# A gated scan after an attention layer: where its roots, step weights and limits are computed

## The chip, the core and the metric

The kernel runs on one core of a Trainium2 chip. A core has a matrix engine (TensorE, PE in the profile, with PEld for its weight loads), a vector engine (VectorE, DVE), an activation engine (ScalarE, ACT), a general engine (GpSimd, POOL), and queues that issue transfers (here SyncE's, SPq, and GpSimd's). Each engine works off its own list in order; engines wait for each other by semaphores. The metric is the device time of one execution in microseconds (us), lower is better. One execution was also recorded by the hardware profiler; the views quoted here are of that one.

## What is computed

Two layers, each added to its input x (8 sequences of 1024 tokens, 512 wide). The first is an attention with 16 heads whose weights are modulated by a condition; it is not touched by the change. The second, cut to what matters:

```python
xr, gate = jnp.split(x @ W_in.T, 2, axis=-1)          # 1024 wide each
xc = silu(conv4(xr + t_emb) + b_conv)                 # causal, four taps, each channel by itself
xn = (xc - mu) / jnp.sqrt(var + 1e-05) * ln_g + ln_b
Bm, Cm, dt = jnp.split(xn @ W_xproj.T, 3, axis=-1)    # 16 states
dt = jnp.tanh(dt @ W_dt.T + b_dt) * 0.01
Ad = 1.0 + dt * (-jnp.tanh(A_log))
Bd = Bm * jnp.minimum(jnp.linalg.norm(xn, axis=-1, keepdims=True), 1.0)
def step(h, inputs):                                  # over 1024 tokens
    ad, bd, xt, ct = inputs
    h = jnp.clip(h * ad[:, :, None] + bd[:, :, None] * xt[:, None, :], -10.0, 10.0)
    return h, jnp.einsum('bd,bdh->bh', ct, h)
y = ys + D * xn
out = x + y * silu(gate) @ W_out.T
```

## The kernel before, in words

**The first layer** (lines 33 to 481) fills the first 3408 us. **The second layer** is `gated_scan`, lines 543 to 1033. The scan state h has 128 partitions (8 sequences times 16 states) and 1024 columns. The kernel keeps h divided by the running product of the decays, so that one step is one VectorE operation (`step`, L933): h plus the step's input, held between two limits that also are divided by that product. The step's input is a row of xn, spread over the 16 states, times a weight of the partition (`st["ws"]`); the output weight is `st["cp"]`.

**Chunks and slots.** Tokens go in 32 chunks of 32 steps; a chunk has two token tiles i = 0, 1 of 16 steps times 8 sequences. All work around the steps is entered in a plan by hand: `at(p0 + k, f, ...)`. For chunk c, p0 is the first step of chunk c-1. So **slot k** below 32 runs in step k of the chunk before, and slots 32 to 63 in the chunk's own steps; the code of one slot is recorded just after `step` of it. Within a slot the work of the older chunk is recorded first, then that of the younger, then `fetch`, `products` and last `weigh`. So step 28 of a chunk holds slot 28 of the next chunk, slot 60 of its own and slot 92 of the one before, and the convolution of the chunk after the next.

**What one chunk does**, by slot: the projection and convolution (`conv_mm`, `conv_in`, `conv_taps`, `conv_out`, slots -12 to 9, that is steps 20 to 31 and 0 to 9; tile `in_ps`, L668 and L672; `xr` L679, `xc` L681, taps L688, `xs` L695); transposes, statistics and the layer norm (`flip_mm` to `scale`, 8 to 17); the root of the variance (`deviation`, 12 and 16); `xt` written to memory (`spill`); norms (`squares`, `lengths`); the projections to B, C and dt (`p_mm` 16, `params` 18, `params_mm` 19 and 21, `params_out` 20 and 22); their spreading by eight small GpSimd transfers (`spread` 24); tanh, running product, weights and limits (`decay` 28); the block of output weights of each tile (`weights` 31 and 41). Then, during its own steps, the gate (`gate_mm`, tile `g_ps`, L823), every four steps the output product (`products`, tile `y_ps`, L920), the gating (`gate_y` L837, `skip` L755), and the last projection (`out_flip` tile `gt_ps`, `out_mm` tile `o_ps`, `out_store`, `out_send`).

**The inputs of the steps.** A tile `xb` holds four steps' inputs. Those of steps 4 to 31 are fetched from memory with a broadcast (`fetch`, 8 transfers of 256 KB, L901). Those of steps 0 to 3 come from TensorE: `fan_mm` (slots 21 and 25) spreads four rows of `xt` into four banks of PSUM for each half of the columns, and `fan_out` (23, 24, 29, 30) copies them to `xb` by ScalarE (L892). Then `weigh(n)` multiplies each step's input by its weight on ScalarE (L911), recorded two steps ahead of its step.

**Buffers.** `xb` has three; h has six, so that step n can write only when `products` has read step n-6; PSUM has two banks for `y_ps` (one tile, 1024 columns) and six, under one tag, for every other product: `in_ps`, `x_ps`, `xp_ps`, `fan_ps`, `g_ps`, `gt_ps`, `o_ps` and more. A product that finds no free bank waits on TensorE until ScalarE or VectorE has read the tile that held it, and all products behind it wait too.

Of the kernel before, what the change touches and what calls it, by code (L numbers as in the profile page):

```python
# [8 lines left out]
F32 = mybir.dt.float32  # L9
BF16 = mybir.dt.bfloat16  # L10
AF = mybir.ActivationFunctionType
ALU = mybir.AluOpType
# [4 lines left out]
P = 128  # L17
B = 8
# [7 lines left out]
TC = 32  # L26
# [516 lines left out]
def gated_scan(ctx, tc, const, tok, x1_d, S, win, tables, w_conv, b_conv, ln_g, ln_b, b_dt, a_log,  # L543
# [69 lines left out]
            ps[:, hf * 512 : (hf + 1) * 512], ident, ident[:, 0:1].to_broadcast([P, 512]), start=True, stop=True  # L613
        )

    eps = wp.tile([P, 1], F32, name="eps_i")
    nc.vector.memset(eps, EPS)
    nc.scalar.activation(na, na, AF.Tanh)
    nc.vector.tensor_scalar_mul(na, na, -0.01)

# [5 lines left out]
    zero = pts[0][:, NX : NX + TC]  # L626
    yws = []
    for n in range(2):
        yw = (tok, wp)[n].tile([P, TT, 4 * B], F32, tag=("sr", "yw")[n], name=f"yw{n}")
        nc.vector.memset(yw, 0.0)  # L630
        yws.append(yw)

# [17 lines left out]
    def at(n, f, *args):  # L650
        if args and args[0] is sts[0] and n < -2:
            n -= 16
        plan.setdefault(n, []).append(lambda: f(*args))
# [73 lines left out]
    def deviation(st, i):  # L727

        rs = st["rs", i] = two.tile([P, 2], F32, name=f"rs{i}")
        mv = st["mv", i]  # L730
        nc.scalar.activation(rs[:, 0:1], mv[:, 1:2], AF.Sqrt, bias=eps)
        nc.vector.reciprocal(rs[:, 0:1], rs[:, 0:1])
        nc.vector.scalar_tensor_tensor(rs[:, 1:2], mv[:, 0:1], -1.0, rs[:, 0:1], ALU.mult, ALU.mult)

    def scale(st, i):
        xt, rs = st["xt", i], st["rs", i]
# [19 lines left out]

    def lengths(st):
        nf = st["nr"] = two.tile([P, NT], F32, name="nr")
        nc.vector.tensor_add(nf, st["nf"][:, :, 0], st["nf"][:, :, 1])
        nc.vector.tensor_scalar_min(nf, nf, 1.0)  # L760
        nc.scalar.activation(nf, nf, AF.Sqrt)

    def params(st, i):
        rs = st["rs", i]
        pt = st["p", i] = pts[i][:, 0:NX]
        add = one.tile([P, NX], F32, name="p_add")
        nc.vector.scalar_tensor_tensor(add, wgs, rs[:, 1:2], wb, ALU.mult, ALU.add)
        nc.vector.scalar_tensor_tensor(pt, st["pt_ps"][:, i, 0:NX], rs[:, 0:1], add, ALU.mult, ALU.add)
        nc.vector.tensor_scalar_mul(pt[:, 0:NS], pt[:, 0:NS], st["nr"][:, i : i + 1])
# [18 lines left out]
    def decay(st):  # L788
        bd, cm, ad = (st["bca"][:, n] for n in range(3))
        nc.scalar.activation(ad, ad, AF.Tanh, bias=bdt)  # L790
        nc.vector.tensor_scalar(ad, ad, na, 1.0, ALU.mult, ALU.add)
        pp = two.tile([P, TC], F32, name="pp")
        nc.vector.tensor_tensor_scan(
            pp, ad, zero, 1.0 if last["p"] is None else last["p"], ALU.mult, ALU.add
        )
        last["p"] = pp[:, TC - 1 : TC]
        lim = st["lim"] = two.tile([P, 2, TC], F32, name="lim")
        nc.vector.reciprocal(lim[:, 0], pp)
        st["ws"] = two.tile([P, TC], F32, name="ws")
        nc.vector.tensor_mul(st["ws"], bd, lim[:, 0])  # L800
        st["cp"] = two.tile([P, TC], F32, name="cp")
        nc.vector.tensor_mul(st["cp"], cm, pp)
        nc.vector.tensor_scalar_mul(lim[:, 1], lim[:, 0], -10.0)
        nc.vector.tensor_scalar_mul(lim[:, 0], lim[:, 0], 10.0)

    def weights(st, i):

        for q in range(4):
            nc.vector.tensor_mul(
                yws[i][:, 4 * q : 4 * q + 4, q * B : (q + 1) * B],  # L810
                my_sb.unsqueeze(1).to_broadcast([P, 4, B]),
                st["cp"][:, i * TT + 4 * q : i * TT + 4 * q + 4].unsqueeze(2).to_broadcast([P, 4, B]),
            )

    def order(st, i):
        xo = st["xo", i] = x1p.tile([P, KH, P], F32, name="x1t")
# [60 lines left out]
    def fan_mm(st, half):  # L877

        for r in range(4):
            ps = st["fan", r] = ps_m.tile([P, 512], F32, tag="mm", name="fan_ps")  # L880
            nc.tensor.matmul(
                ps, sel[32 * r : 32 * r + 32], st["xt", 0][32 * r : 32 * r + 32, half * 512 : (half + 1) * 512],
                start=True, stop=True,
            )

    def fan_out(st, c, half, rs):
        if half == 0 and rs[0] == 0:
            st["xb"] = xbp.tile([P, 4, DI], F32, name="xb")
            for r in range(4):
                xbs[c * TC + r] = st["xb"][:, r]  # L890
        for r in rs:
            nc.scalar.copy(st["xb"][:, r, half * 512 : (half + 1) * 512], st.pop(("fan", r)))  # L892

    def fetch(g):

# [17 lines left out]
    def products(g):  # L913

        c, t = divmod(4 * g, TC)
        i, q = divmod(t // 4, TT // 4)
        st = sts[c]
        for hf in range(2):
            for r in range(4):
                nc.tensor.matmul(  # L920
                    st["y", i][32 * r : 32 * r + 32, hf * 512 : (hf + 1) * 512],
                    yws[i][:, 4 * q + r, :],
                    hs[4 * g + r][:, hf * 512 : (hf + 1) * 512],
                    start=False, stop=(q == 3), skip_group_check=True,
                )
        for r in range(4):
            del hs[4 * g + r]
# [12 lines left out]
    for c in range(NCH):  # L940
        st, n0 = sts[c], c * TC
        p0 = n0 - TC
        if c > 0:
            at(p0 + -20 if c > 1 else -34, load_x1, st, c)
        at(p0 + -15, begin, st)
        for k in range(KI):
            at(p0 + -12 + 2 * k, conv_mm, st, k)
            at(p0 + -11 + 2 * k, conv_in, st, k)
            at(p0 + -10 + 2 * k, conv_taps, st, k, (0,))
            at(p0 + -9 + 2 * k, conv_taps, st, k, (1,))  # L950
            at(p0 + -8 + 2 * k, conv_taps, st, k, (2,))
            at(p0 + -7 + 2 * k, conv_out, st, k)
        at(p0 + 8, flip_mm, st, 0, 0)
        at(p0 + 8, flip_mm, st, 0, 1)
        at(p0 + 11, stats, st, 0, 0)
        at(p0 + 11, stats, st, 0, 1)
        at(p0 + 11, center, st, 0)
        at(p0 + 12, deviation, st, 0)
        at(p0 + 14, scale, st, 0)
        at(p0 + 17, spill, st, 0)  # L960
        at(p0 + 15, squares, st, 0)
        at(p0 + 35, skip, st, 0)
        at(p0 + 12, flip_mm, st, 1, 0)
        at(p0 + 12, flip_mm, st, 1, 1)
        at(p0 + 15, stats, st, 1, 0)
        at(p0 + 15, stats, st, 1, 1)
        at(p0 + 15, center, st, 1)
        at(p0 + 16, deviation, st, 1)
        at(p0 + 17, scale, st, 1)
        at(p0 + 28, spill, st, 1)  # L970
        at(p0 + 18, squares, st, 1)
        at(p0 + 51, skip, st, 1)
        at(p0 + 21, fan_mm, st, 0)
        at(p0 + 23, fan_out, st, c, 0, (0, 1))
        at(p0 + 24, fan_out, st, c, 0, (2, 3))
        at(p0 + 25, fan_mm, st, 1)
        at(p0 + 29, fan_out, st, c, 1, (0, 1))
        at(p0 + 30, fan_out, st, c, 1, (2, 3))
        at(p0 + 16, p_mm, st)
        at(p0 + 18, lengths, st)  # L980
        at(p0 + 18, params, st, 0)
        at(p0 + 19, params_mm, st, 0)
        at(p0 + 20, params_out, st, 0)
        at(p0 + 18, params, st, 1)
        at(p0 + 21, params_mm, st, 1)
        at(p0 + 22, params_out, st, 1)
        at(p0 + 24, spread, st)
        at(p0 + 28, decay, st)
        at(p0 + 31, weights, st, 0)
        at(p0 + 41, weights, st, 1)  # L990
        at(p0 + 34, order, st, 0)
        at(p0 + 36, gate_mm, st, 0, 0)
        at(p0 + 42, gate, st, 0, 0)
        at(p0 + 41, gate_mm, st, 0, 1)
        at(p0 + 43, gate, st, 0, 1)
        at(p0 + 50, gate_y, st, 0)
        at(p0 + 62, out_flip, st, 0, 0)
        at(p0 + 64, out_copy, st, 0, 0)
        at(p0 + 65, out_mm, st, 0, 0)
        at(p0 + 63, out_flip, st, 0, 1)  # L1000
        at(p0 + 65, out_copy, st, 0, 1)
        at(p0 + 69, out_mm, st, 0, 1)
        at(p0 + 73, out_store, st, 0)
        at(p0 + 76, out_send, st, c, 0)
        at(p0 + 46, order, st, 1)
        at(p0 + 49, gate_mm, st, 1, 0)
        at(p0 + 51, gate, st, 1, 0)
        at(p0 + 61, gate_mm, st, 1, 1)
        at(p0 + 64, gate, st, 1, 1)
        at(p0 + 65, gate_y, st, 1)  # L1010
        at(p0 + 68, out_flip, st, 1, 0)
        at(p0 + 68, out_copy, st, 1, 0)
        at(p0 + 77, out_mm, st, 1, 0)
        at(p0 + 70, out_flip, st, 1, 1)
        at(p0 + 77, out_copy, st, 1, 1)
        at(p0 + 78, out_mm, st, 1, 1)
        at(p0 + 80, out_store, st, 1)
        at(p0 + 91, out_send, st, c, 1)
# [2 lines left out]
            at(4 * g - 9 if g > 2 else -25, fetch, g)  # L1021
        at(4 * g + 4, products, g)
    for n in range(S):
        at(n - WA, weigh, n)

    sts[0]["x1"] = x1_now
    last["h"] = hp.tile([P, DI], F32, tag="h", name="h")
# [117 lines left out]
```

## Time and profile before

| | us |
|---|---|
| time before, median of 3 runs | 5712.75 (5705.14 to 5713.35) |
| the profiled execution's own time | 5708.03 |
| its span, first to last instruction | 5706.3 |
| first layer, up to the first scan step | 3408.0 |
| a chunk of 32 steps, mean of chunks 0 to 30 | 71.39 |
| one undisturbed chunk (the 19th, from 4764.57) | 71.08 |

The page gives busy time as a share of the whole span, over both layers. Only the second layer is of interest here, and there the engines stand at: PE 98%, DVE 94%, ACT 89%, transfers 88% (the stretch from 4408 to 5408 us: 981.53, 944.41 and 894.25 us of 1000). GpSimd is busy 123 us of those 1000. A line of the timeline reads: start, length, engine, line of the code, operation, out<-in, shape, count; in brackets the idle time before it and what ended that.

### The profile page before, as it was taken

How to read it: one execution, taken by the hardware profiler on the slowest of the kernel's cores; microseconds unless marked ns; L12 is line 12 of the kernel's file. 1: busy time of each engine (PE TensorE's matmuls, PEld its weight loads, DVE VectorE, ACT ScalarE, POOL GpSimd, SP SyncE). 2: the span in 40 equal slices, each digit the busy share in tenths (PEclk: the TensorE clock that was granted, in tenths of full speed). 3: DMA queues.
4: the chain of work that ended last, by engine and by line, in shares of the span. 5: the costliest groups of instructions: out<-in, count | busy, mean ns of one | idle time of the engine just before them, and what ended most of it. 6: DMA issues, size and time to landing. Idle time of an engine off the chain costs nothing.

```text
span 5706.3 us, 113668 instructions
## 1 busy us (share of the span) xinstructions
PE 5525.4 (97%) x43312; PEld 3178.8 (56%) x43312; DVE 4382.9 (77%) x6874; ACT 3959.9 (69%) x6995; POOL 1540.4 (27%) x1667
## 2 busy tenths in 40 slices
PE   7999999999999999999999989999999999999998
PEld 4565656656556556656556555555555555555553
DVE  4666666766766766766666659999999999999996
ACT  5565655655655655655655558898988888888886
POOL 2343433433434434434433310111111111111111
PEclk9999999999999999999999989999999999999999
DMA  2102212112112112112021248888888888888886
GB/s 83 35 24 64 53 44 67 31 55 57 31 58 53 38 50 67 24 53 71 18 65 41 71 123 233 236 238 237 238 238 234 237 235 238 235 238 236 238 238 188
DMA packets 377216, 714.85 MB, mean 125 GB/s; under 512 B 198320, under 2 KB 280512, under 8 KB 347488
## 3 DMA queue, kind: packets, MB, share of 16 engines
q1 hardware_dynamic: 346704, 684.81, 44.4%
q0 software_dynamic: 29968, 22.77, 1.5%
q8 instruction: 344, 5.64, 0.4%
q14 instruction: 200, 1.64, 0.1%
HBM read 596.66 MB, written 83.89 MB: 119 GB/s over the span
## 4 chain that ended last, share of the span: by engine, by line
PE 63%; DMA 15%; DVE 9%; ACT 8%; issue 3%; SPq 2%; POOL 0%; DVEq 0%; ACTq 0%; POOLq 0%
PE mm_ps L130 17%; PE t_ps L296 15%; DMA xb<-xd 10%; PE s_ps L286 9%; PE t_ps L303 8%; DVE h L933 4%; PE in_ps L668 4%; PE y_ps L920 3%; ACT xb L911 2%; PE g_ps L823 2%; SPq L901 2%; DMA out<-o_sb 2%; ACT pr L457 2%; PE o_ps L860 1%; DMA xd<-xt 1%
## 5 line engine op out<-in xcount | busy, mean ns | idle before, releaser
L447 DVE TENSOR_REDUCE nmax<-s_ps 128x1 f32<-128x1024 f32 x1024 | 1206.2, 1220 | 460.7 <-PE s_ps L289 459.9
L454 ACT COPY pT<-t_ps 128x512 f32<-128x512 f32 x1024 | 550.3, 589 | 1298.9 <-PE t_ps L296 1298.4
L933 DVE CUSTOM_DVE_ANT_0 h<-h,xb,lim 128x1024 f32<-128x1024 f32 x1024 | 1373.5, 1341 | 90.0 <-ACT xb L911 41.2
L296 PEld LDWEIGHTS t_ps<-ident,pr 128*128 128x128 f32 x8192 | 912.2, 141 | 658.9 <-issue 491.7
L911 ACT ACTIVATE xb<-xb,ws 128x1024 f32<-128x1024 f32 x1024 | 1177.8, 1164 | 60.2 <-DMA xb<-xd 45.0
L457 ACT ACTIVATE pr<-s_ps,nmax 128x1024 f32<-128x1024 f32 x1024 | 1139.5, 1127 | 5.0 <-DVE nmax L447 4.8
L296 PE MATMUL t_ps<-ident,pr 128*128 128x128 f32 x8192 | 1096.9, 277 | 28.4 <-ACT pT L454 24.7
L476 POOL TENSOR_SCALAR pr<-pr,rinv 128x1024 f32<-128x1024 f32 x512 | 572.2, 1118 | 130.0 <-DVE rinv L475 123.0
L286 PE MATMUL s_ps<-kT,qT 32*128 32x512 f32 x2048 | 596.0, 641 | 2.5 <-ACT pr L457 1.7
L289 PE MATMUL s_ps<-k,q 32*128 32x512 f32 x2048 | 578.0, 640 | 1.1 <-DMA q<-qT 1.1
L462 POOL TENSOR_SCALAR pr<-pr,rinv 128x1024 f32<-128x1024 f32 x256 | 286.8, 1121 | 1070.7 <-PE t_ps L296 751.4
L920 PE MATMUL y_ps<-h,yw 128*32 128x512 f32 x4096 | 527.3, 610 | 36.6 <-DVE y_ps L755 31.6
L303 PEld LDWEIGHTS t_ps<-pT,vt 128*32 128x32 f32 x16384 | 433.9, 110 | 207.6 <-DVE rinv L470 112.9
L303 PE MATMUL t_ps<-pT,vt 128*32 128x128 f32 x16384 | 506.9, 274 | 19.1 <-DVE pT L468 12.3
L471 POOL TENSOR_SCALAR pr<-pr,rinv 128x1024 f32<-128x1024 f32 x256 | 286.2, 1118 | 844.6 <-DVE rinv L470 795.7
L668 PE MATMUL in_ps<-x,win 128*128 128x256 f32 x2048 | 492.2, 386 | 3.8 <-ACT xb L892 3.8
L823 PE MATMUL g_ps<-win,x1t 128*128 128x512 f32 x1024 | 470.5, 602 | 4.0 <-ACT x1t L818 3.6
L860 PE MATMUL o_ps<-wout,xt 128*128 128x512 f32 x1024 | 458.5, 595 | 0.0
L872 POOL DMA_DIRECT2D out<-o_sb x256 | 151.0, 595 | 1053.0 <-ACT o_sb L866 953.3
L668 PEld LDWEIGHTS in_ps<-x,win 128*128 128x128 f32 x2048 | 376.9, 193 | 95.2 <-ACT xb L892 26.2
L786 POOL DMA_DIRECT2D bca<-few x256 | 129.1, 515 | 1019.1 <-ACT few L779 1013.5
L468 DVE COPY pT<-t_ps 128x512 f32<-128x512 f32 x512 | 352.0, 687 | 56.1 <-PE t_ps L296 55.6
(157 smaller groups left out, 6975.4 us busy)
## 6 DMA issues: line engine op xcount, KB each, us to landing
xb<-xd SPq DMA_DIRECT2D x1792, 256.0 KB
xd<-xt SPq DMA_DIRECT2D x64, 512.0 KB
q<-qT SPq DMA_DIRECT2D x128, 128.0 KB
xr<-in_xT SPq DMA_DIRECT2D x64, 256.0 KB
xu_d<-xr SPq DMA_DIRECT2D x64, 256.0 KB
xr<-xu_d SPq DMA_DIRECT2D x64, 256.0 KB
x_d<-xr SPq DMA_DIRECT2D x64, 256.0 KB
out<-o_sb POOLq DMA_DIRECT2D x256, 64.0 KB, 6.0
```

What stands on the lines that cost most here:

```text
L130: nc.tensor.matmul(ps, w, x, start=(k == 0), stop=(k == KH - 1))
L286: nc.tensor.matmul(s_ps[i][:, 0:HW], st["q"][r, qc], st["k"][r, 0:HW], start=True, stop=True)
L289: nc.tensor.matmul(s_ps[i][:, HW:S], st["q2"][r, qc], st["k2"][r], start=True, stop=True)
L296: nc.tensor.transpose(ps[:, j], pr[:, c0 : c0 + P], ident)
L303: nc.tensor.matmul(av[r], vt[:, kt, r], pT[:, i, kt], start=(kt == 0), stop=(kt == KT - 1), skip_group_check=True,)
L447: nc.vector.tensor_reduce(nmax[i], s_ps[i], AX.X, ALU.max, negate=True)
L457: nc.scalar.activation(fresh[i], s_ps[i], AF.Exp, bias=nmax[i], accum_out=rsum[i])
L668: nc.tensor.matmul(ps, win[kk][:, k * P : (k + 1) * P], st["x1"][:, kk].rearrange("p b t -> p (b t)"), start=(kk == 0), stop=False,)
L823: nc.tensor.matmul(ps, st["xo", i][:, k], win[k][:, DI + half * 512 : DI + (half + 1) * 512], start=(k == 0), stop=(k == KH - 1),)
L911: nc.scalar.mul(xbs[n], xbs[n], sts[c]["ws"][:, t : t + 1])
L920: nc.tensor.matmul(st["y", i][32 * r : 32 * r + 32, hf * 512 : (hf + 1) * 512], yws[i][:, 4 * q + r, :], hs[4 * g + r][:, hf * 512 : (hf + ...
L933: nc.vector._custom_dve(dve_ops.TENSOR_ADD_SAT, out=h, in0=last["h"], in1=xbs.pop(n), s0=lim[:, 0, t : t + 1], s1=lim[:, 1, t : t + 1],)
```

## The change

The roots go from ScalarE (square root) and VectorE (reciprocal) to GpSimd (add, then a power of -0.5 or 0.5 with a second operand from a small tile `halves`). The second column of `rs` (minus the mean times the inverse deviation) is made in `params`, which moves from slot 18 to 20, its product and copies from 19 and 20 to 21 and 22. The two limits are made by ScalarE from the reciprocal of the product. Each tile's block of output weights is written by one VectorE operation in place of four, in another layout. The inputs of a chunk's first four steps are multiplied by their weights while they are copied from PSUM, and `weigh` leaves these steps out; because the weights must be there, the two `fan_mm` move from slots 21 and 25 to 28 and 30, and the four `fan_out` from 23, 24, 29 and 30 to 29 to 32.

```diff
-        nc.scalar.activation(rs[:, 0:1], mv[:, 1:2], AF.Sqrt, bias=eps)
-        nc.vector.reciprocal(rs[:, 0:1], rs[:, 0:1])
-        nc.vector.scalar_tensor_tensor(rs[:, 1:2], mv[:, 0:1], -1.0, rs[:, 0:1], ALU.mult, ALU.mult)
+        nc.gpsimd.tensor_scalar(rs[:, 0:1], mv[:, 1:2], EPS, None, ALU.add)
+        nc.gpsimd.tensor_tensor(rs[:, 0:1], rs[:, 0:1], halves[:, 0:1], ALU.pow)
...
     def lengths(st):
         nf = st["nr"] = two.tile([P, NT], F32, name="nr")
-        nc.vector.tensor_add(nf, st["nf"][:, :, 0], st["nf"][:, :, 1])
-        nc.vector.tensor_scalar_min(nf, nf, 1.0)
-        nc.scalar.activation(nf, nf, AF.Sqrt)
+        nc.gpsimd.tensor_tensor(nf, st["nf"][:, :, 0], st["nf"][:, :, 1], ALU.add)
+        nc.gpsimd.tensor_scalar(nf, nf, 1.0, None, ALU.min)
+        nc.gpsimd.tensor_tensor(nf, nf, halves[:, 1:3], ALU.pow)
 
     def params(st, i):
...
+        nc.vector.scalar_tensor_tensor(rs[:, 1:2], st["mv", i][:, 0:1], -1.0, rs[:, 0:1], ALU.mult, ALU.mult)
...
-        nc.vector.reciprocal(lim[:, 0], pp)
+        rp = two.tile([P, TC], F32, name="rp")
+        nc.vector.reciprocal(rp, pp)
...
-        nc.vector.tensor_scalar_mul(lim[:, 1], lim[:, 0], -10.0)
-        nc.vector.tensor_scalar_mul(lim[:, 0], lim[:, 0], 10.0)
+        nc.scalar.mul(lim[:, 0], rp, 10.0)
+        nc.scalar.mul(lim[:, 1], rp, -10.0)
 
     def weights(st, i):
 
-        for q in range(4):
-            nc.vector.tensor_mul(
-                yws[i][:, 4 * q : 4 * q + 4, q * B : (q + 1) * B],
-                my_sb.unsqueeze(1).to_broadcast([P, 4, B]),
-                st["cp"][:, i * TT + 4 * q : i * TT + 4 * q + 4].unsqueeze(2).to_broadcast([P, 4, B]),
-            )
+        nc.vector.tensor_mul(
+            yws[i][:, :, 0 : TT * B].rearrange("p q (r w) -> p q r w", r=4)[:, :, :, 0:B],
+            my_sb.unsqueeze(1).unsqueeze(1).to_broadcast([P, 4, 4, B]),
+            st["cp"][:, i * TT : (i + 1) * TT].rearrange("p (q r) -> p q r", r=4).unsqueeze(3).to_broadcast([P, 4, 4, B]),
+        )
...
-            nc.scalar.copy(st["xb"][:, r, half * 512 : (half + 1) * 512], st.pop(("fan", r)))
+            nc.scalar.mul(st["xb"][:, r, half * 512 : (half + 1) * 512], st.pop(("fan", half, r)), st["ws"][:, r : r + 1])
...
-        at(p0 + 21, fan_mm, st, 0)
-        at(p0 + 23, fan_out, st, c, 0, (0, 1))
-        at(p0 + 24, fan_out, st, c, 0, (2, 3))
-        at(p0 + 25, fan_mm, st, 1)
-        at(p0 + 29, fan_out, st, c, 1, (0, 1))
-        at(p0 + 30, fan_out, st, c, 1, (2, 3))
         at(p0 + 16, p_mm, st)
         at(p0 + 18, lengths, st)
-        at(p0 + 18, params, st, 0)
-        at(p0 + 19, params_mm, st, 0)
-        at(p0 + 20, params_out, st, 0)
-        at(p0 + 18, params, st, 1)
+        at(p0 + 20, params, st, 0)
+        at(p0 + 21, params_mm, st, 0)
+        at(p0 + 22, params_out, st, 0)
+        at(p0 + 20, params, st, 1)
         at(p0 + 21, params_mm, st, 1)
         at(p0 + 22, params_out, st, 1)
         at(p0 + 24, spread, st)
+        at(p0 + 28, fan_mm, st, 0)
         at(p0 + 28, decay, st)
+        at(p0 + 29, fan_out, st, c, 0, (0, 1))
+        at(p0 + 30, fan_out, st, c, 0, (2, 3))
+        at(p0 + 30, fan_mm, st, 1)
+        at(p0 + 31, fan_out, st, c, 1, (0, 1))
+        at(p0 + 32, fan_out, st, c, 1, (2, 3))
...
     for n in range(S):
-        at(n - WA, weigh, n)
+        if n % TC >= 4:
+            at(n - WA, weigh, n)
```

## The prediction, made before the result was known

> **What bounds the kernel now.** The change touches the second layer alone, so I read one undisturbed chunk there, the 19th: first the busy time of that stretch, then TensorE's timeline, then VectorE's. The busy time (columns: stretch, length, then PE, PEld, DVE, ACT, POOL, granted clock, share and rate of the transfers):
>
> ```profile
> 4764.57:4835.65 71.08, 69.97 (x362) 37.14 (x358) 67.47 (x101) 63.77 (x112) 8.74 (x16) 1.00 0.88 238
> ```
>
> TensorE has 1.1 us of 71.08 free, VectorE 3.6, ScalarE 7.3. No engine has room, so the order decides, not a share. TensorE's timeline from there on:
>
> ```profile
> 4810.88 1.92 PE L920 MATMUL y_ps<-h,yw 128*32 128x512 f32 x16 [0.84 <-DVE y_ps L755]
> ...
> 4824.96 2.29 PE L920 MATMUL y_ps<-h,yw 128*32 128x512 f32 x16
> 4827.18 3.70 PE L823 MATMUL g_ps<-win,x1t 128*128 128x512 f32 x8
> 4830.72 0.60 PE L843 MATMUL gt_ps<-ident,gate 128*128 128x128 f32 x4
> 4831.15 1.89 PE L668 MATMUL in_ps<-x,win 128*128 128x256 f32 x8
> 4832.88 0.27 PE L672 MATMUL in_ps<-hot_b,cond_b 128*128 128x256 bf16 x1
> 4832.99 0.60 PE L843 MATMUL gt_ps<-ident,gate 128*128 128x128 f32 x4
> 4833.43 1.89 PE L668 MATMUL in_ps<-x,win 128*128 128x256 f32 x8
> 4835.16 0.27 PE L672 MATMUL in_ps<-hot_b,cond_b 128*128 128x256 bf16 x1
> 4835.36 1.92 PE L920 MATMUL y_ps<-h,yw 128*32 128x512 f32 x16
> ...
> 4853.74 1.92 PE L920 MATMUL y_ps<-h,yw 128*32 128x512 f32 x16
> ```
>
> The reader is to see one idle stretch with a releaser (0.84, VectorE's L755 of step 19) and after it 44.8 us without a gap, to the product of slot 40 (4853.74, ended 4855.66). VectorE, same chunk:
>
> ```profile
> 4784.69 1.34 DVE L933 CUSTOM_DVE_ANT_0 h<-h,xb,lim 128x1024 f32<-128x1024 f32 x1 [0.27 <-ACT gate L831]
> ...
> 4805.29 1.22 DVE L837 TENSOR_TENSOR gate<-y_ps,gate 128x1024 f32<-128x1024 f32 x1
> 4806.42 0.15 DVE L759 TENSOR_TENSOR nr<-nf 128x2 f32<-128x2 f32 x1
> 4806.60 0.17 DVE L760 TENSOR_SCALAR nr<-nr 128x2 f32<-128x2 f32 x1
> 4806.68 0.26 DVE L767 SCALAR_TENSOR_TENSOR p_add<-wgs,rs,wb 128x48 f32<-128x48 f32 x1
> ...
> 4808.24 1.34 DVE L933 CUSTOM_DVE_ANT_0 h<-h,xb,lim 128x1024 f32<-128x1024 f32 x1
> 4809.50 1.23 DVE L755 TENSOR_TENSOR y_ps<-xt,d_bc 128x1024 f32<-128x1024 f32 x1
> ...
> 4827.59 0.24 DVE L791 TENSOR_SCALAR bca<-bca,na 128x32 f32<-128x32 f32 x1 [0.65 <-ACT bca L790]
> ...
> 4828.19 0.35 DVE L798 RECIPROCAL lim<-pp 128x32 f32<-128x32 f32 x1
> ```
>
> Step 10 (4784.69) starts as the product of slot 40 of its chunk ends: step n needs the h buffer of step n-6, which that product reads. In the next chunk it starts at 4855.77, 0.11 after 4855.66. So the chunk is a **loop**: VectorE from step 10 to the end of L755 (4784.69 to 4810.73, 26.04 us), 0.15 to TensorE, its run without a gap (44.78), 0.11 back: 71.08. What is taken from VectorE between steps 20 and 9 is outside this loop.
>
> **The change, part by part.** I follow the loop of the changed kernel, with the durations above. The order of its instructions on each engine and the banks its tiles get are read from the two built programs.
>
> *A, step 10 to L755.* Step 18 loses L759, L760 and both `params`: all from 4806.42 to 4808.24, -1.82. The roots of steps 12 and 16 lie in waits of VectorE for its own last step (a bare step takes 1.51, these took 1.52): 0. A = 26.04 - 1.82 = 24.22. Cover: GpSimd must have the roots by L737, which starts 4.2 us (second tile: 4798.63 to 4802.83) and 5.6 us (first) after its mean and variance. The trace has no GpSimd operation on one column; rows: 128x1024 in 1118 ns and 128x512 in 762, so about 406 ns for no column; two inputs of 512 columns took 1269; a memset of one column about 100. Bounds for add and power together 0.2 to 2.5; I take 0.8, nearest to the fixed part: hidden. A power beyond 3.4 us would show. `lengths` has 5 us for three operations: hidden too. The queue ahead of them is `out_send` (four issues of 0.6), over by step 10.
>
> *B, L755 to the reciprocal of the product.* Before: 4810.73 to 4828.54, 17.81. Step 20 took 1.48 and gets both `params` (1.56, from 4806.68 to 4808.24) and two more L733 in a dependent chain (0.2 each) after 1.26 of its own: 3.22, so +1.74. Gone: steps 24 to 27 waited for ScalarE's L911 (0.47, 0.27, 0.26 idle; with steps back at 2.05, 1.65, 2.05: -1.26), because the `fan_out` of slots 23 and 24 stood ahead; and the wait for tanh (-0.72 with its start). B = 17.81 + 1.74 - 1.98 = 17.57. The eight small transfers land about 13.5 us after L755, tanh is needed at 16; a slower landing costs what passes that.
>
> *C, the new wait.* The weights exist only now, and on ScalarE these stand in order after the reciprocal: two limits, `weigh` of step 30, `fan_out` r=0, 1, the two `xs`, `xr`, `xc`, `weigh` of step 31, `fan_out` r=2, 3, then the first `fan_out` of the second half. On TensorE, slot 29 has `g_ps` and slot 30 `gt_ps` in two of the six banks; the second `fan_mm` of slot 30 gets the bank of `fan_ps` r=1, that of `in_ps`, and those of r=2 and r=3; the `in_ps` behind it gets the bank of the second half's own r=0. So TensorE stands still until that `fan_out` is done, and everything behind stands with it. ScalarE's increments, from starts that follow each other: L911 1.04, L892 0.47, plus 0.1 for a scale from a tile (L681 has two such and takes 0.46 where L679 takes 0.26), so 0.57; `xs` 0.65 for two; limits 0.15 each (L790, 0.21, less its operand). C = 0.1 + 0.3 + 1.04 + 2x0.57 + 0.65 + 0.26 + 0.46 + 1.04 + 3x0.57 + 0.14 (tail) = 6.84. That is 24.41 after L755. TensorE comes there at about 21.4: product of slot 28 over at 16.4, `g_ps` 3.5, `gt_ps` 0.44, `fan_mm` 1.07; it waits 3.
>
> *D, from there to the product of slot 32.* `in_ps` 2.00; ScalarE's `xr` and `xc` 0.86 before the next `in_ps` gets their bank; that one 1.93; 0.2 of handing over: 4.99.
>
> *E*, that product to step 10: 4835.36 to 4855.77, 20.41; VectorE regains its place there, waiting for the banks at steps 2, 6 and 10 as before.
>
> Sum: 24.22 + 17.57 + 6.84 + 4.99 + 20.41 = 74.03 against 71.08, **+2.95 per chunk**. Thirty of the 31 changes of chunk have a convolution beside them: +88.5. The waits that other chunks show at step 16 (ScalarE's root behind L866; step 16 is 1.69 in the mean and 1.52 here) go: 30 x 0.17 = -5. Start and last chunk: 0.
>
> What hides: merged `weights` (four start 0.10 apart, 0.49 in all; one of 128 columns some 0.3), limits and `weigh` of four steps save VectorE 0.7 and ScalarE 4.7 per chunk, all between steps 28 and 9, where the loop runs over TensorE: 0. The fetch of steps 4 to 7 gets its buffer four steps earlier: 0 or a gain, no transfer being last here.
>
> ScalarE also loses two table loads per chunk, 1283 ns each, with 0.02 idle before them. [...]
>
> [...]
>
> **The rivals.** (1) *Faster*: ScalarE reaches the second half before TensorE does, so the loop keeps only the gains. It decides at B + C below 21.4, that is C below 3.8. The loop is then A 24.22, 0.15, 16.3 from the product of slot 20 to the end of that of slot 28, 8.11 + 1.07 to that of slot 32, and 20.41: 70.26, -0.82, so -25 - 5: 5678. For it: ScalarE is 4.7 us a chunk lighter; against: its order is fixed, and C is a chain of waits, not a load. (2) *No change*: TensorE's wait costs only what A gives back: 5700 to 5720. (3) *Roots late*: a power of 5 us makes L737 of the second tile 2.4 late, +72: 5863.
>
> **The numbers.** Profiled span 5706.3 + 88.5 - 5 = 5789.8; 1.7 lie around the span (5708.03), so 5791. The runs shown have a median of 5712.75, five above the profiled one, which the measurement moves by anyway; 0.2% is about what one can tell from no change. Range: per chunk +1.6 (`fan_out` without the 0.1, a wait in D that overlaps) gives 5751; +4.2 (the small transfers landing 1 us late, a stall at step 31) gives 5828. Chances: forecast 0.82, roots late 0.05, no change 0.04, faster 0.09.
>
> **What would show it.** Right: TensorE idle some 3 us before `fan_ps` r=1 to 3 and the `in_ps` behind, released by ScalarE's `fan_out`, and again about 0.5 before the next `in_ps`; L755 of step 19 some 24.2 after step 10; chunks of 74. Wrong: chunks near 70 with no such wait (B or C far shorter), or L737 waiting for GpSimd (step A).

## The result, and the profile after

The changed kernel takes **5935.58 us** (median of 4 runs, 5929.28 to 5956.73) against 5711.07 of the kernel before in the same rounds: ratio **1.0401**, 95% interval 1.0378 to 1.0425. The forecast was 5791 (5751 to 5828): the sign and the mechanism came, the size did not. The profiled execution has a span of 5930.7 us against 5706.3: a chunk takes 78.70 us in the mean and not 71.39 (31 x 7.31 = 227); the first scan step comes 5.4 us earlier, and the last chunk with the end takes 3.1 us longer.

The same loop as in the forecast, measured over chunks 3 to 28 of both traces (means, us):

| term | before | forecast | after |
|---|---|---|---|
| A, step 10 to the end of L755 | 26.32 | 24.22 | 24.65 |
| B, to the reciprocal of the product | 17.94 | 17.57 | **19.34** |
| C, to the end of the first weighed copy of the second half | - | 6.84 | 6.71 |
| D, to the product of slot 32 | 6.74 (C and D together) | 4.99 | **7.89** |
| E, to step 10 | 20.43 | 20.41 | 20.42 |
| chunk | 71.43 | 74.03 | 79.01 |

One chunk of the changed kernel, from step 10 to step 10 (columns: stretch, length, PE, PEld, DVE, ACT, POOL, granted clock, share and rate of the transfers), in the view of the prediction's first line:

```profile
5002.03:5082.25 80.22, 76.62 (x359) 39.54 (x360) 66.67 (x88) 58.44 (x105) 11.61 (x24) 0.96 0.79 211
```

There, TensorE was busy for all but 1.1 us and its granted clock was 1.00; here 3.6 us are free and the clock is 0.96 in the mean. VectorE in this chunk:

```profile
5002.03 1.34 DVE L934 CUSTOM_DVE_ANT_0 h<-h,xb,lim 128x1024 f32<-128x1024 f32 x1 [0.51 <-PE y_ps L921]
...
5024.97 1.23 DVE L755 TENSOR_TENSOR y_ps<-xt,d_bc 128x1024 f32<-128x1024 f32 x1
...
5046.14 0.24 DVE L792 TENSOR_SCALAR bca<-bca,na 128x32 f32<-128x32 f32 x1 [2.78 <-ACT bca L791]
...
5046.74 0.35 DVE L800 RECIPROCAL rp<-pp 128x32 f32<-128x32 f32 x1
```

Step 10 to the end of L755 is 24.17 us, as forecast. Then L792 waits 2.78 us for tanh (0.65 before), whose inputs, the small transfers to `bca`, have come late. From 8 to 16 us after the end of L755, when these transfers run, all transfers together take a share of 0.33 before and of 1.01 now (last column but one; the prediction's chunk of the kernel before, then this one):

```profile
4818.73:4826.73 8.00, 8.00 (x54) 4.34 (x46) 7.00 (x9) 8.00 (x15) 3.31 (x6) 1.00 0.33 91
```

```profile
5034.20:5042.20 8.00, 8.00 (x57) 4.24 (x50) 7.60 (x12) 4.54 (x8) 3.03 (x6) 1.00 1.01 243
```

TensorE from the product of slot 28 to that of slot 32:

```profile
5040.84 2.33 PE L921 MATMUL y_ps<-h,yw 128*32 128x512 f32 x16
5043.40 3.70 PE L824 MATMUL g_ps<-win,x1t 128*128 128x512 f32 x8 [0.23 <-ACT xc L682]
5049.14 0.66 PE L844 MATMUL gt_ps<-ident,gate 128*128 128x128 f32 x4 [2.03 <-ACT xb L893]
5049.72 1.12 PE L882 MATMUL fan_ps<-xt,sel 32*128 32x512 f32 x2
5051.07 4.26 PE L882 MATMUL fan_ps<-xt,sel 32*128 32x512 f32 x6 [0.23 <-ACT xc L682]
5055.26 3.50 PE L669 MATMUL in_ps<-x,win 128*128 128x256 f32 x8
5058.60 0.27 PE L673 MATMUL in_ps<-hot_b,cond_b 128*128 128x256 bf16 x1
5058.71 0.60 PE L844 MATMUL gt_ps<-ident,gate 128*128 128x128 f32 x4
5059.80 1.99 PE L669 MATMUL in_ps<-x,win 128*128 128x256 f32 x8 [0.49 <-ACT xc L682]
```

In the kernel before, this run had no gap. Now TensorE stands for `fan_out` (L893) as forecast. The four `fan_ps` products of one half are eight records (x8); they take 1.14 us where nothing holds them, and here they spread over 5.6, most of which the page counts as busy. The `in_ps` behind them takes 3.50 us, the next one 1.99. The granted clock tells why (columns: stretch, length, PE busy, clock, transfers):

```profile
5046.00:5050.00 4.00, 1.97 (x8) 1.00 0.24 93
5050.00:5052.00 2.00, 1.77 (x4) 0.88 0.26 104
5052.00:5058.00 6.00, 6.00 (x12) 0.50 0.65 164
5058.00:5062.00 4.00, 3.51 (x21) 0.96 1.01 254
```

Here the clock is 1 until TensorE has stood still, then half for 6.83 us (from 5051.52), then 1 again. In the trace's record of the clock the share is 1 or 0.5 only, and the stretches at 0.5 are multiples of 3.41 us (3.41, 6.83 or 10.24; but for the last one of a run). In the second layer they make 39.8 us before (9 stretches) and **239.5 us** after (43), most of them at the stall around steps 31 and 0. So there were two suspects for what the forecast lacks: transfers that come late (B), and the clock (D).

### The profile page after: what moved, and what is told of

It reads as the page before. It is cut to its first block, busy times and chain, and to the rows that moved or that the text cites. A ratio compares the mean times of both kernels' runs of the same rounds, so it can differ in the third digit from the quotient of the medians.

```text
span 5930.7 us, 113466 instructions
## 1 busy us (share of the span) xinstructions
PE 5714.4 (96%) x43312; PEld 3249.9 (55%) x43312; DVE 4355.7 (73%) x6491; ACT 3780.5 (64%) x6770; POOL 1640.1 (28%) x1891
## 5 line engine op out<-in xcount | busy, mean ns | idle before, releaser
L912 ACT ACTIVATE xb<-xb,ws 128x1024 f32<-128x1024 f32 x896 | 1006.7, 1144 | 68.5 <-DMA xb<-xd 54.0
L669 PE MATMUL in_ps<-x,win 128*128 128x256 f32 x2048 | 545.4, 415 | 17.2 <-ACT xc L682 8.4
L921 PE MATMUL y_ps<-h,yw 128*32 128x512 f32 x4096 | 542.7, 618 | 12.3 <-DVE h L934 6.2
L669 PEld LDWEIGHTS in_ps<-x,win 128*128 128x128 f32 x2048 | 405.7, 206 | 199.3 <-issue 58.5
L689 DVE SCALAR_TENSOR_TENSOR xc<-xr,cw,xc 128x256 f32<-128x256 f32 x768 | 352.8, 479 | 120.7 <-ACT xc L682 119.5
```

The costliest lines, as they stand in the source:

```text
L669: nc.tensor.matmul(ps, win[kk][:, k * P : (k + 1) * P], st["x1"][:, kk].rearrange("p b t -> p (b t)"), start=(kk == 0), stop=False,)
L912: nc.scalar.mul(xbs[n], xbs[n], sts[c]["ws"][:, t : t + 1])
L921: nc.tensor.matmul(st["y", i][32 * r : 32 * r + 32, hf * 512 : (hf + 1) * 512], yws[i].rearrange("p q w -> p (q w)")[:, (4 * q + r) * 4 * ...
```

## The experiments

All were timed against the kernel before, whose median was 5710 to 5712 us in each set; the diffs are against the changed kernel unless said otherwise.

**1. The change without its fan part** (`rest_only`): `fan_mm` and `fan_out` at the slots of before, all steps weighed.

```diff
-            nc.scalar.mul(st["xb"][...], st.pop(("fan", half, r)), st["ws"][:, r : r + 1])
+            nc.scalar.copy(st["xb"][...], st.pop(("fan", half, r)))
...
-        at(p0 + 28, fan_mm, st, 0)
+        at(p0 + 21, fan_mm, st, 0)
...
-        at(p0 + 30, fan_mm, st, 1)
+        at(p0 + 25, fan_mm, st, 1)
```

> The whole change but its fan part: fan products and copies in their old slots, copies without weights, weighing of all steps. Theory (all of the loss is in the fan part, what follows from the late weights): the loop keeps A at 24.2 and runs over TensorE from the product of slot 20, which then waits some 1 us at slot 28 for step 27 (params now stand in step 20); chunks of 70.4 to 70.6, about 5690 us, a little faster than before. Rival (the roots on GpSimd, or params in step 20, cost by themselves): slower than before, 5730 or more, with step 10 to the end of L755 well above 24.2.

Measured: 5714.06 us, ratio 1.0007 (0.9998 to 1.0017); 27.5 us at a clock of 0.5. Without the fan part the loss is gone. The gain expected of the rest did not come: A is 24.2 us (1.9 less), but from L755 to the end of the product of slot 28 it takes 18.25 us and not 16.53. The `params` that left step 18 stand in step 20 (3.22 us and not 1.48), and ahead of steps 25 to 27 VectorE still waits 1.0 us in all for ScalarE's L912, as before (0.47, 0.27 and 0.26); in the changed kernel, where that wait is gone, the same stretch takes 17.0. Nor was there room for much (columns as in the first line above; the kernel before, then this one):

```profile
3500.00:5600.00 2100.00, 2057.89 (x10497) 1090.13 (x10499) 1982.06 (x2907) 1874.27 (x3254) 253.91 (x464) 1.00 0.88 237
```

```profile
3500.00:5600.00 2100.00, 2072.52 (x10454) 1091.86 (x10452) 1955.96 (x2538) 1778.07 (x3151) 342.33 (x672) 1.00 0.87 235
```

TensorE is busy 98 and 98.7% of the stretch: of a chunk some 1.4 and 0.9 us are free, whatever is taken from VectorE (94 to 93%) and ScalarE (89 to 85%). That this alone would have stopped a gain is not shown.

**2. The buffer asked for earlier** (`early_buffer`): in the changed kernel, sixteen broadcast transfers of `fetch` are issued in a row, from 1.1 us before the end of L755 to some 14 after it; before, eight were, and the next eight only from 14.6. The buffer for the first four steps is now taken in slot 29 and not 23, so `fetch` finds one free.

```diff
+    def hold(st, c):
+        st["xb"] = xbp.tile([P, 4, DI], F32, name="xb")
...
+        at(p0 + 23, hold, st, c)
```

> The changed kernel, but the buffer of the first four steps' inputs is taken in slot 23 as before, so the fetch for steps 4 to 7 again starts after step 27. Transfer theory (that fetch, four steps earlier, runs beside the eight small transfers and makes them land at 17.6 us after L755 in the mean in place of 13.2, so that tanh is late): landing back near 13.5, B from 19.3 to about 17.6, so 1.8 us per chunk, 54 us: about 5880. Rival (the small transfers are late for another reason, such as the output's transfers in the same queue): landing and time stay, 5935.

Measured: 5931.27 us, ratio 1.0392, and nothing moved: the sixteen transfers still start at -1.1, `bca` lands 17.5 us after L755. A tile that nobody writes holds no buffer here (in experiment 4, which writes one column, the transfers do move), so the run tests nothing.

**3. TensorE kept busy with products of 32 rows** (`warm`, and `early_warm` with edit 2 added): the first three replicating products of the second half, behind which TensorE would wait for a bank, are repeated five, four and one times, ten more in all.

```diff
+            for _ in range((5, 4, 1, 0)[r] * half + 1):
                 nc.tensor.matmul(ps, sel[32 * r : 32 * r + 32], ...)
```

> The changed kernel with ten repeated fan products (0.27 us each, the same result written again) put where TensorE stands still in the second half: after r=0 five, after r=1 four, after r=2 one. Clock theory (TensorE's clock is granted at 0.50 for some 7 us after it has stood still, which makes the products behind take 7.9 us in place of 5): clock stays near 1.0, D back to about 5, 2.9 us per chunk, 88 us: about 5850. Rival (these products are long because of waits that the trace counts as work): D stays at 7.9 or grows by the repeats, 5935 to 6010.

> Both of the others together: buffer taken in slot 23, and ten repeated products. If the clock and the small transfers are all that the forecast missed, the loop is 24.2 + 17.6 + 6.7 + 5.0 + 20.4 = 73.9 and the time about 5790, what the forecast said. Rival (something else is late too): above 5830.

Measured: 6193.87 and 6187.52 us, both at a ratio of 1.084. The time at 0.5 grew from 239.5 us to 454.6 and 482.4; the extra products run at half clock too, so C and D became 10.8 and 11.35 us in `warm`. TensorE in one chunk of `warm`, and its clock (stretch, length, PE busy, clock, transfers):

```profile
5040.34 10.69 PE L883 MATMUL fan_ps<-xt,sel 32*128 32x512 f32 x28
```

```profile
5040.00:5044.00 4.00, 4.00 (x14) 1.00 0.25 102
5044.00:5052.00 8.00, 8.00 (x24) 0.62 0.95 248
```

The profile shows no gap, and the clock falls all the same: these products of 32 rows fill the page's busy share and do not hold the clock.

**4. The buffer really taken in slot 24** (`early_touch`): `hold` also writes one column.

```diff
     def hold(st, c):
...
+        nc.scalar.copy(st["xb"][:, 0, 0:1], halves[:, 0:1])
...
+        at(p0 + 24, hold, st, c)
```

> The changed kernel, in which the buffer of the first four steps' inputs is really taken in slot 24: it is allocated there, and ScalarE writes one column of it at once (128x1), so that the transfers of the steps 4 to 7 get the next buffer and can begin only when step 27 has let it go. Transfer theory: in the changed kernel 16 broadcast transfers run in a row from 1.1 us before the end of L755, since the buffer is free too soon; the small transfers to bca land behind them 17.6 us after the end of L755 and not 13.2, and the reciprocal ends 19.34 us after it. Here only 8 run ahead, bca lands 13.5 to 14.5 us after L755, the reciprocal ends after about 17.8, and 31 x 1.5 = 47 us go: 5885 us (5870 to 5900). The terms behind the reciprocal stay (6.7 and 7.9 us), and so does the time at a granted clock of 0.5, 43 stretches and 239 us. Rival (the small transfers are late for another reason, such as the later params of step 20): bca still lands at 17 to 18 us, 5930 to 5940 us.

Measured: 5872.64 us, ratio 1.0277 (1.0259 to 1.0294): 63 us less than the changed kernel. `bca` lands 13.9 us after L755 (17.6 without the edit) and B is 18.02. B is still 0.45 above the forecast, and that is ScalarE's: in the 9 chunks in which its weighings between L755 and tanh wait less than 0.1 us for their fetch, B is 17.57 in the mean, the forecast's number; in the other 17 they wait 0.3 to 3.06 us, and B goes up to 20.02 with that wait. What was not expected: the time at 0.5 also fell, to 160 us, and D to 7.36. With B shorter, TensorE stands less. In four of the 26 chunks the clock does not fall at all around the stall; TensorE in one of them, where it does not stand ahead of `gt_ps` as it did above (2.03 us; the last row is cut by the window's end):

```profile
5237.18 0.60 PE L844 MATMUL gt_ps<-ident,gate 128*128 128x128 f32 x4
5237.71 1.67 PE L882 MATMUL fan_ps<-xt,sel 32*128 32x512 f32 x4
5239.87 1.70 PE L882 MATMUL fan_ps<-xt,sel 32*128 32x512 f32 x4 [0.49 <-ACT xb L895]
5241.50 1.99 PE L669 MATMUL in_ps<-x,win 128*128 128x256 f32 x8
5243.33 0.27 PE L673 MATMUL in_ps<-hot_b,cond_b 128*128 128x256 bf16 x1
5243.44 0.60 PE L844 MATMUL gt_ps<-ident,gate 128*128 128x128 f32 x4
5244.53 1.78 PE L669 MATMUL in_ps<-x,win 128*128 128x256 f32 x7 [0.49 <-ACT xc L682]
```

This chunk is 24.15 + 17.53 + 6.71 + 5.59 + 20.30 + 0.11 = 74.4 us long; the forecast's was 74.03. The only difference of size is in D, 5.59 and not 4.99: the fifth copy ends at 5240.97, and the forecast lets `in_ps` start there; but the replicating product of row 3, which got its bank only at 5240.4, runs until 5241.57, and `in_ps` starts behind it, 0.53 later. (The `gt_ps` lies beside ScalarE's `xr` and `xc` and costs nothing.)

**5. Whole products in the stall** (`warm_full`): two ahead of the second half's first product, one ahead of its second, into the bank that the real product then overwrites.

```diff
+            for _ in range((2, 1, 0, 0)[r] * half):
+                nc.tensor.matmul(ps, win[0][:, 0:P], win[1][:, 0:512], start=True, stop=True)
             nc.tensor.matmul(ps, sel[32 * r : 32 * r + 32], ...)
```

> The changed kernel, in which TensorE runs products of the whole array (128 rows, 512 columns, of two input weights, their result unused) in the time in which it stands still: two ahead of the first replicating product of the second half and one ahead of the second, each into the bank that the real product then writes over. [...] Whole products are counted: the time at 0.5 in the second layer falls from 239 us to under 100, the term from the fifth weighed copy to the product of step 32 falls from 7.9 to about 5.2 us, and the time by 31 x 2.7 = 84 us to about 5850 (5835 to 5875). Rival (the 7.9 us are the waits between TensorE, VectorE and ScalarE in the steps 0 and 1, whatever the clock): the term stays at 7.9 or grows by up to three products, 2.6 us: 5930 to 6015 us.

Measured: 5901.85 us, ratio 1.0336 (1.0320 to 1.0353). The time at 0.5 fell from 239.5 to 62 us, and D from 7.89 to 6.38 although TensorE has three products more to do. What was expected of the clock came. The time lies between the two ranges: the gain is 34 us and not 84, since D stays well above 5.2 (it is 5.59 where the clock does not fall, experiment 4) and B grew by 1.3 us (`bca` lands 18.6 us after L755). B is that of the profiled execution, the slowest of the four (5917 us).

**6. Both edits** (`touch_warm`).

> The two edits together: the buffer of the first four inputs taken in slot 24 with a write of one column, and three whole products in TensorE's stall. If both theories hold, the gains add: 31 x (1.5 + 2.7) = 130 us, 5805 us (5785 to 5835), close to the forecast for the changed kernel, with the reciprocal 17.8 us after the end of L755 and the product of step 32 some 12 us after the reciprocal. If one theory fails, the time is that of the other run within 10 us; if the two share a cause (the clock falls because the inputs come late), the gains do not add and the time is above 5840.

Measured: 5842.25 us, ratio 1.0225 (1.0210 to 1.0241). The gains are 63 and 34 us alone and 93 together. That is less than expected, and by the expectation's own line (above 5840) the two could share a cause. By the terms they do in part: with the earlier buffer B is 18.02 and not 19.34, with the products or without, but by itself it also takes 0.53 from D, since with B shorter the clock falls less (160 us at 0.5 and not 239.5, experiment 4); both together take 1.64 from D. That the times add so well is partly chance, as the 1.3 us that the products alone add to B are missing here. The second layer from 3500 to 5600 us in the changed kernel and in this one:

```profile
3500.00:5600.00 2100.00, 2036.45 (x9539) 1054.65 (x9531) 1773.26 (x2314) 1551.14 (x2760) 320.88 (x621) 0.95 0.80 215
```

```profile
3500.00:5600.00 2100.00, 2067.92 (x10090) 1067.22 (x10088) 1846.53 (x2414) 1626.36 (x2907) 327.67 (x644) 1.00 0.82 223
```

The clock is back at 1.00 from 0.95. A chunk is 75.89 us, 1.86 above the forecast: D 1.26 (0.60 as in the chunk above, and the rest perhaps the filling product ahead of the second bank, which is not shown), B 0.45, A 0.12.

**7. The fan part alone on the kernel before** (`fan_only`; the diff is that of the change, its fan lines alone).

> The kernel before with the fan part alone: the replicating products in slots 28 and 30, their copies weighed by the output of decay, no weighing of the first four steps; roots on ScalarE, params in step 18, limits on VectorE and four weight operations as before. Theory (all of the loss is the fan part's, and what the rest gains in VectorE's stretch it gives back in steps 20 to 28): about the changed kernel's time, 5925 us (5900 to 5945), with 26.0 us from step 10 to the end of L755. Rival (the rest's shorter stretch, 24.2 us, is a gain that only the kernel with the fan in time keeps): the loss is larger by 1.8 us a chunk, 5985 us.

Measured: 5979.75 us, ratio 1.0469 (1.0453 to 1.0484): the rival's number, 44 us above the changed kernel. A is 26.4 us here. So what the rest of the change takes from VectorE is a real gain, 1.4 us a chunk, in a kernel with the late fan, and none in one without it, where the stretch behind L755 gives it back (experiment 1).

**8. The fan by rows** (`rows`): rows 0 and 1 in slots 28 to 30, rows 2 and 3 behind the product of slot 32. The buffer is taken in slot 24 with a written column, as in experiment 4.

```diff
-        at(p0 + 30, fan_mm, st, 1)
-        at(p0 + 31, fan_out, st, c, 1, (0, 1))
-        at(p0 + 32, fan_out, st, c, 1, (2, 3))
+        at(p0 + 33, fan_mm, st, (2, 3))
+        at(p0 + 33, fan_out, st, c, 2)
+        at(p0 + 34, fan_out, st, c, 3)
```

> The changed kernel with the fan cut by rows and not by halves, so that TensorE has no bank to wait for: the replicating products of rows 0 and 1 (both halves, four banks) in slot 28, their weighed copies in 29 and 30; those of rows 2 and 3 in slot 33, behind the products of slot 32, their copies in 33 and 34, ahead of the steps 34 and 35; the buffer taken in slot 24 with a write of one column. Theory: what the fan costs is TensorE's stall ahead of the second half and what follows from it (the term from the reciprocal to the product of step 32, 14.6 us against 7.36 without the fan part; the clock of 0.5). It goes: that term is 7 to 7.6 us, the time at 0.5 in the second layer under 60 us (28 without the fan part), the stretch from the product of step 32 to that of step 8 grows by the four products, 1.1 us, and a chunk takes 24.2 + 18.0 + 7.4 + 21.4 + 0.1 = 71.1 us: 5700 us (5685 to 5730). Rival (the first four steps' inputs are late in whatever order, since eight copies of 0.7 us stand between the reciprocal and step 35): the steps 34 and 35 hold up the product of step 36 by 2 to 3 us, 5770 to 5810 us.

Measured: 5793.32 us, ratio 1.0137 (1.0123 to 1.0151): 142 us less than the changed kernel, of which 63 are experiment 4's. The first half came nearly as expected: the reciprocal to the product of slot 32 takes 7.8 us and not 14.6, and the time at 0.5 is 43 us. The rival takes the rest; VectorE's step 2:

```profile
4965.50 1.34 DVE L937 CUSTOM_DVE_ANT_0 h<-h,xb,lim 128x1024 f32<-128x1024 f32 x1 [4.47 <-ACT xb L896]
```

It waits 4.47 us for its weighed input, since the products of rows 2 and 3 stand behind 4.0 us of `o_ps`; the run from the product of slot 32 to that of step 8 is 23.8 us and not 20.3.

**9. VectorE relieved of the params** (`rows_gp` and `rest_gp`): the offset by GpSimd, the weighing with the lengths by ScalarE, everything one slot earlier.

```diff
+        nc.gpsimd.tensor_scalar(sh, wgs, st["mv", i][:, 0:1], st["rs", i][:, 0:1], ALU.mult, ALU.mult)
+        nc.gpsimd.tensor_tensor(sh, wb, sh, ALU.subtract)
...
+        nc.scalar.mul(pt[:, 0:NS], pt[:, 0:NS], st["nr"][:, i : i + 1])
...
-        at(p0 + 21, params_mm, st, 0)
+        at(p0 + 20, params_mm, st, 0)
```

> As the fan by rows, and the params taken off VectorE: of eight operations per chunk two stay there (268 ns each); the offset is made on GpSimd in slot 18 (a product with two scalars and a subtraction of 128x48), the weighing with the lengths by ScalarE; params, their transposition, their copies and the small transfers one slot earlier (19, 20, 21, 23). VectorE loses 1.85 - 0.54 = 1.3 us of a stretch in which it has nothing to wait for, and the small transfers, one step earlier, land ahead of step 28. Theory (the stretch from step 10 to the product of step 28 is VectorE's): 1.3 to 2 us a chunk less than the fan by rows alone, 5640 to 5660 us. Rival (ScalarE or the small transfers set the end of that stretch): within 15 us of the fan by rows alone.

> The changed kernel without its fan part (5714 us by itself), with the same edit of the params. Theory: the stretch is VectorE's and 1.3 us shorter per chunk, 5675 us (5655 to 5690). Rival: ScalarE's weighing in the steps 24 to 27, for which VectorE waits some 1.5 us per chunk without the fan part, is late anyway, and takes the 1.3 us back: 5705 to 5715 us. Between the two the fan by rows, which has four weighings fewer and no copies in the steps 23 and 24, would gain more than this one.

Measured: 5885.01 us (ratio 1.0302, 1.0288 to 1.0316) and 5817.43 us (1.0182, 1.0168 to 1.0196): 92 and 103 us *worse* than without the edit, which neither theory had. In slot 20 the transposes of the params stand ahead of the product of slot 20 on TensorE, and they now wait for GpSimd and ScalarE in turn. Steps 19 and 20 of `rest_gp`:

```profile
4946.51 1.34 DVE L936 CUSTOM_DVE_ANT_0 h<-h,xb,lim 128x1024 f32<-128x1024 f32 x1
4946.97 2.27 POOL L765 TENSOR_SCALAR p_add<-wgs,mv,rs 128x48 f32<-128x48 f32 x1
...
4947.77 1.23 DVE L755 TENSOR_TENSOR y_ps<-xt,d_bc 128x1024 f32<-128x1024 f32 x1
...
4949.60 0.37 POOL L765 TENSOR_SCALAR p_add<-wgs,mv,rs 128x48 f32<-128x48 f32 x1
...
4950.31 0.55 PE L777 MATMUL xp_ps<-ident,pt 128*128 128x128 f32 x3 [2.78 <-ACT pt L772]
```

TensorE idles 2.78 us there, and step 22 then waits 3.33 us for the h buffer that the delayed product reads. The edit was badly placed, so it does not tell what VectorE's 1.3 us would be worth; that stays open.

**10. No fan at all** (`no_fan`): the first four steps are fetched like the others, and all steps are weighed by `weigh`.

```diff
-        if g % (TC // 4) > 0:
-            at(4 * g - 9 if g > 2 else -25, fetch, g)
+        at(4 * g - 9 if g > 2 else -25, fetch, g)
```

> The changed kernel without any fan: the first four steps' inputs come by eight broadcast transfers in slot 23 of the chunk before, as all others do, and are weighed by ScalarE two steps ahead (four weighings of 1.13 us in place of eight copies of 0.7). TensorE has idle time of 0.9 us in a chunk of 71.6 without the fan part, so that only less work for TensorE can shorten the chunk; here it loses eight replicating products, 1.14 + 1.34 us. Theory (TensorE's own work is the bound): 31 x 2 to 2.5 us less than 5714, 5637 to 5655 us. Rival (the transfers are next: they are busy for 0.87 of the second layer with seven groups of eight per chunk, eight groups make 0.99): no gain or a loss, 5700 to 5790 us, with steps that wait for their fetch.

Measured: 5811.04 us, ratio 1.0182 (1.0162 to 1.0202): the rival, and beyond its range. ScalarE's `weigh` between 3500 and 5600 us (busy, mean ns, idle before it and for what):

```profile
L912 ACT ACTIVATE xb<-xb,ws 128x1024 f32<-128x1024 f32 x898 | 1020.7, 1150 | 383.7 <-DMA xb<-xd 352.4 <-issue 17.1 <-DVE h L934 11.4
```

It waits 352 us for fetches (33 in the kernel before), with the transfers' share at 0.94. The fan by TensorE is what keeps the transfers off the path. No version here beats the kernel before.

## Why the prediction failed in size

- **A held**: 24.17 us in the median, 24.22 forecast. The roots on GpSimd stay hidden: an add of one column took 219 ns and the power 561, 0.78 together where 0.8 was taken; L737 never waits for them, so the rival "roots late" did not come. In 8 of 26 chunks A is 25.7, since the clock falls a second time, at steps 16 and 17, and the product of slot 16 comes late.
- **B failed by 1.77 us**, at the sentence "The fetch of steps 4 to 7 gets its buffer four steps earlier: 0 or a gain, no transfer being last here." The earlier fetch runs just when the eight small transfers to `bca` need the queues: in the 8 to 16 us after L755 the transfers' share is 0.94 to 1.02, against 0.33 to 0.36 before. `bca` lands at 17.6 and not 13.2 us, past the 16 at which the text itself said that tanh needs it; in 15 of 26 chunks tanh starts 0.2 us after the last landing, and before the change never less than 2.4 us after it. The range allowed for 1 us of this. Experiment 4 puts the fetch back: 1.32 us of the 1.77 go, and part of D with them; the other 0.45 are ScalarE's waits for its fetches, as shown there.
- **C held**: 6.71 against 6.84, with 0.57 for the increment of a weighed copy as worked out.
- **D failed by 2.90 us**, the largest error. 0.60 comes without any fall of the clock (5.59 in the chunks of experiment 4 where it stays up): the sum let `in_ps` start with the fifth copy's end and left out that the second half's last product, which waits for a bank, too, is still to run. The other 2.30 go with the clock: the step took the durations of TensorE's rows as fixed, though they were measured in a stream without a gap, and the change makes a gap. Experiments 5 and 6 show it by putting the clock back, with D at 6.38 and 6.25 although TensorE has more to do.
- **E held**: 20.42 against 20.41. The terms missed add up: 0.43 + 1.77 - 0.13 + 2.90 + 0.01 = 4.98 us a chunk.
- The rivals "faster" and "no change" did not come; C was a chain of waits, as argued. That what A gives back would count, which the sum assumed, holds with the fan part (1.4 us a chunk, experiment 7) and not without it (experiment 1).

In the chunk shown, the clock fell to 0.5 after 2.0 us of standstill and 2.4 us with only the four transposes of `gt_ps` (0.66 us) and a few 32-row products, and rose again after 6.83 us, two of the 3.41; in the chunk of `warm` it fell with no gap in the profile (0.62 in the mean from 5044 to 5052). The forecast worked out 3 us of waiting, and left the rows behind it at the durations they had without a gap.

VectorE's operations beside the new ones of GpSimd did not get longer, and A is as worked out without such a cost. The roots run beside L723, and the operations of `lengths` mostly beside L838; L723 takes 0.75 us in the mean before and after, L838 1.22, `step` 1.34. GpSimd's own did: L760 (a minimum) takes 0.23 us beside L838, and in 9 of 31 chunks, in which it starts beside `step`, 1.1 to 1.2 us, while `step` keeps its 1.34. Experiment 9 shows a second row of this kind: GpSimd's L765 took 2.27 us beside a step and L755, and 0.37 us beside L771; the step and L755 kept their 1.34 and 1.23. What held L760 and L765 up is not shown.

Open: the 0.66 us that D still has in experiment 6 beyond 5.59, and how far the fan by rows could go with its second products ahead of `o_ps`.

## What to carry to other kernels

Here a wait put into an engine that was 98% busy was paid in full, and on TensorE a second time, by the products behind it that ran at half clock (3.50 us and not 1.99 for the first `in_ps`): price a new stall there with slower rows behind it. When a buffer is taken later, look which transfer gets the one that is now free, and which small transfer then stands behind it. Time taken from one stretch of an engine is worth nothing where the next stretch gives it back (experiment 1: A lost 1.9 us, the stretch behind it grew by 1.7).

## What the hardware did that was not expected

- Replicating products of 32 rows did not hold the clock, even without a gap: with ten more a chunk the time at 0.5 went from 239.5 to 454.6 us; three of 128 rows a chunk brought it to 62.
- A stall can hide in the busy share: six records of fan products counted 4.26 us, eight unhindered ones 1.14.
- The eight small transfers to `bca` took 8.3, 12.5 and 13.5 us in the mean from the first issue to the last landing (the kernel before, the changed one, `warm_full`), and 8.8 with the earlier fetch put back (`early_touch`).
- GpSimd's power took 561 ns on one column and 713 on two.
